# The last attention pair by query halves, and another order of the first and last chains

## The chip, the cores and the metric

The kernel runs on one core of one Trainium2 chip. The metric is the device time of one execution in microseconds. The times shown are of three runs; the profile is of one further execution, with its own time.

A core has five engines that run beside each other and are tied by semaphores: PE (matrix products; its weight loads are listed as PEld), DVE (vector), ACT (scalar functions and copies), POOL (here powers and scalings) and SP (here only the issue of transfers). ACT issues transfers too. Each engine works through its own instructions in order.

## The reference

Eight sequences x[b] of 512 rows with 128 features. All is float32.

```python
x = x + 0.5 * ffn(layernorm(x))
x = x + attention(layernorm(x))
x = x + 0.5 * ffn(layernorm(x))

# attention: 16 heads, rank 64
scores = einsum('bthr,buhr->bthu', x @ Q, x @ K) / sqrt(128)
attn = softmax(scores, axis=3)
return einsum('bthu,bud,hde->bte', attn, x, VO)

# ffn: three blocks, each weight is dequantized 4 bit plus a LoRA product
for blk in range(3):
    y = qlora_linear(h, 2 * blk)
    y = gelu(layernorm(y) * gamma + beta)
    h = qlora_linear(y, 2 * blk + 1) + h
```

## The kernel before

**Pairs and turns.** A batch's 512 rows are four chunks of 128 (c = 0 to 3). Heads go in pairs: 8 pairs per batch, 64 pairs in all, and two pairs make a turn (`lay_turn`), so there are 32 turns. A turn has a nominal length of 32 (`SUP`). For each chunk of queries of a pair: scores on PE (L753), row maxima on DVE (L760), exponentials on ACT with their sums (L765), reciprocals (L772), division by the sums on POOL for one head (L777) and on ACT for the other (L779), and a transpose on DVE (L787) that turns 32x32 blocks into the tile `tr`. The blocks are then moved to their places by 16 transfers from `tr` to `eT` (`exchange`, L802), each 32 partitions by 4 KB. In the last pair (number 63) the odd ones go out on ACT's queue, all others on SP's. The products of `eT` with the values `v` (`attend`, L823) add up in PSUM in `acc0` and `acc1`, over all pairs of a batch; one such product, 128 by 512, is two instructions on PE. They run one or two turns later than the scores of their pair.

**Feed-forward between the turns.** The parts before and after attention of the other batches are laid into the turns by `Unit` and `Block`: a LayerNorm of four chunks at a time (`Norm`: stats L353 and L355 on DVE, root L361 on POOL, scale L366 on DVE, transposes L335 on PE), then for each of three blocks `first` (L388), `biased` (L395 and the stats), root, scale, transposes, `gelu` (L413), `second` (L420), `add` (L426), and at the end `ffn_add` (L436) with the store of the batch.

**The two bare ends.** Where no attention runs beside them, batch 0's first feed-forward part and batch 7's second are done as four `Part` chains, one per chunk: per layer stats (L462), mean (L466), root (L470, POOL), scale (L474), transpose (L479), gelu (L519), and the products into PSUM rows `y` (L490), where all biases and blocks add up. `sum` (L540) ends a part. At the start each part then goes on through a second LayerNorm, its transpose (`keep`, L1025) and its k and q (L700, L706) to the scores of turn 0. Ahead of the end's parts stand copies of `acc0` to `oT` (L1138), transposes (`pot`, L1155) and an addition to x (L537, `xadd`). Pair 61, 62 and 63 are the last three pairs; pair 62's products run after the last turn's scores, then pair 63's.

**The order.** Nothing is scheduled at run time. Every step is put into a list by `at(t, fn)`, the list is sorted by t, and each engine's instructions keep this order by dependencies that the last loop adds. So a number t is a place in the queues, not a time that anything waits for. `START` and `END` hold the t of the bare chains' steps, one number for each of the four parts, relative to `T0` and `E`. A step waits where its data or its buffer are not ready, and all behind it on that engine wait too. PSUM has eight banks of 2 KB per partition, handed out by name (`tag`) from a pool; there are three pools one after the other, and `psum.next` goes to the next.

**Around the change at the end.** With L the place of the last turn, the order on PE is: pair 61's last products and the values of pairs 62 and 63, the transposes `pother` of the half of batch 7's attention sum that lies in `acc1` (its copy on ACT is L854, its addition to x on DVE L860), eight products of pair 62 with `second` and `first` of batch 6's last blocks between them (L + 42 to 45), the transposes of the last block (L + 45.5), four products of pair 63 (L + 58), `second`, three products, the transposes of `ffn_add`, the last product, and then the parts.

**Around the change at the start.** `Unit(0, 1)` and `Unit(0, 2)` are the first feed-forward parts of batches 1 and 2. `lay_start` gets the places of their stats, root, scale, transposes and copy; turn 0 begins at 0.

Of the kernel before, what the change touches and what calls it, by code (L numbers as in the profile page):

```python
# [10 lines left out]
F32 = mybir.dt.float32  # L11
# [7 lines left out]
def kernel(  # L19
# [26 lines left out]
    nc = tc.nc  # L46
# [498 lines left out]
    def part_banks(f):  # L545

        ys = [bank(f"py{f}_{i}", f"y{i}") for i in range(NC)]
        p = [bank(f"pp{f}_{i}", f"g{i}") for i in range(2)]
        return [(ys[i], [p[i % 2][:, 2 * (i // 2) + j, :] for j in range(2)]) for i in range(NC)]
# [107 lines left out]
    class Pair:  # L657
# [123 lines left out]
        def turn(self, c):  # L781

            if c == 0:
                self.tr = work.tile(
                    [P, Q4, 2 * NC, NC, 32], F32, tag="tr", name=f"tr{self.name}", bufs=2
                )
            nc.vector.transpose(  # L787
                self.tr[:, :, :, c, :],
                self.e[c].rearrange("p h (k j r) -> p j (h k) r", j=Q4, r=32),
            )  # L790

        def exchange(self):
# [4 lines left out]
            for s in range(Q4):  # L797
                for i in range(Q4):
                    j = (i + s) % Q4

                    queue = nc.scalar if self.last and i % 2 else nc.sync
                    queue.dma_start(  # L802
# [6 lines left out]
        def attend(self, j, k, tiles):  # L809
# [10 lines left out]
            end = self.g == HP - 1 and k == NC - 1  # L820
# [30 lines left out]
    def lay_other_sum(b, t):  # L851

        a = work.tile([P, NC, P], F32, tag="oT", name=f"other{b}", bufs=2)
        at(t, lambda: nc.scalar.copy(  # L854
            a.rearrange("p c (i q) -> p i c q", q=32), by_chunks(accs[b][1])
        ))

        def add():
            p = transposed(a, f"pother{b}", "g0")
            nc.vector.tensor_tensor(xs[b], xs[b], p, ALU.add)  # L860

        at(t + 3.9, add)
# [3 lines left out]
    def lay_turn(s):  # L866
# [20 lines left out]
        at(t + (24.5 if not last else 22.9), two[1].exchange)  # L887
# [37 lines left out]
    def store(b):  # L925
# [4 lines left out]
        "statsn": (3.79, 3.60, 5.17, 5.36),  # L930
        "meann": (4.09, 3.98, 5.55, 5.66),
        "rootn": (4.71, 4.16, 5.73, 6.28),
        "scalen": (5.74, 4.90, 6.34, 6.89),
        "turnn": (6.12, 5.89, 6.98, 7.83),
        "start": (6.43, 6.20, 7.29, 8.18),
        "bias0": (5.68, 5.78, 6.00, 5.57),
        "y0": (6.77, 6.55, 7.94, 8.49),
        "stats0": (7.35, 7.16, 8.66, 8.91),
        "mean0": (7.65, 7.54, 9.10, 9.51),
        "root0": (8.27, 7.72, 9.28, 9.83),  # L940
        "scale0": (9.18, 8.33, 9.89, 10.44),
        "turn0": (10.10, 8.92, 12.12, 11.47),
        "gelu0": (10.55, 9.23, 12.43, 11.78),
        "bias1": (9.99, 8.81, 10.42, 10.88),
        "second": (11.04, 10.21, 12.92, 12.27),
        "sadd": (11.46, 10.77, 13.36, 12.70),
        "y1": (11.90, 11.26, 13.90, 13.14),
        "stats1": (12.32, 11.79, 14.32, 13.69),
        "mean1": (12.62, 12.09, 14.62, 14.21),
        "root1": (12.82, 12.27, 14.94, 14.39),  # L950
        "scale1": (13.88, 13.03, 15.55, 15.08),
        "turn1": (14.48, 13.47, 16.10, 15.62),
        "gelu1": (14.79, 13.78, 16.41, 15.93),
        "bias2": (14.81, 13.58, 15.99, 15.52),
        "in2": (14.59, 13.68, 16.20, 15.73),
        "y2": (15.29, 14.27, 17.07, 16.42),
        "stats2": (15.88, 14.70, 17.55, 16.84),
        "mean2": (16.43, 15.00, 17.85, 17.14),
        "root2": (16.61, 15.49, 18.03, 17.32),
        "scale2": (17.22, 16.10, 18.64, 17.93),  # L960
        "turn2": (17.88, 16.64, 19.12, 18.37),
        "gelu2": (18.19, 16.95, 19.43, 18.68),
        "bias3": (17.66, 17.28, 19.66, 19.02),
        "in3": (17.77, 16.96, 19.77, 18.91),
        "o31": (17.98, 16.75, 19.45, 18.48),
        "o32": (18.69, 17.44, 19.92, 19.23),
        "sum": (19.16, 18.26, 20.42, 19.79),
        "statsa": (19.60, 18.97, 20.86, 20.23),
        "meana": (20.12, 19.49, 21.32, 20.75),
        "roota": (20.30, 19.67, 21.50, 20.93),  # L970
        "scalea": (21.05, 21.40, 22.11, 21.67),
        "turna": (21.44, 21.79, 22.59, 22.06),
        "keep": (21.75, 22.52, 22.95, 22.37),
        "k": (22.16, 22.91, 23.26, 22.70),
        "kk": (22.80, 23.42, 23.67, 23.12),
        "sc75": 4.40, "w0": 4.62, "w12": 6.01, "w345": 7.73, "cols": 4.70, "colsk": 5.01,
        "gb": 7.73, "gbk": 8.33, "lbA": 3.00, "lbAk": 3.52, "lbB": 6.23, "lbBk": 6.75,
        "wt0": 5.25, "wt0k": 5.77, "wt12": 7.09, "wt12k": 7.93, "wt345": 9.02, "wt345k": 10.19,
        "nat3": 11.58, "nat3a": 12.13, "x21": 12.49, "x21k": 12.91, "cst": 10.71, "cstk": 10.97,
        "qt": 8.34, "qtk": 8.65, "kt": 8.70, "ktk": 9.01, "q": 22.38, "qk": 23.27,  # L980
    }
    T0 = -23.98
# [71 lines left out]
    m.lay_start((-3.3, -2.9, -1.6, 1.95, 5.3), "g0")  # L1054
# [5 lines left out]
    m.lay_start((-1.5, -1.4, 6.2, 9.5, 9.5), "g1")  # L1060
# [4 lines left out]
    for b in range(B):  # L1065
# [10 lines left out]
        if b < B - 1:  # L1076
# [6 lines left out]
                ("first", 2): (44.4, 44.5, 45.0, 45.4),  # L1083
                ("second", 2): (13.5, 13.6, None, 27.7, 27.8),
                "end": 28.9,
# [128 lines left out]
```

## Time and profile before

| | us |
|---|---|
| median of 3 runs | 1083.18 |
| lowest, highest | 1082.44, 1084.1 |
| profiled execution, its time | 1082.74 |
| profiled execution, span from first to last instruction | 1080.9 |
| mean granted clock of PE | 0.997 of full |

| stretch of the trace (us) | PE busy | DVE busy | ACT busy | POOL busy | granted clock |
|---|---|---|---|---|---|
| 22.00 to 25.10 | 3.10 | 2.83 | 1.37 | 1.69 | 1.00 |
| 25.10 to 27.10 | 0.05 | 1.94 | 0.00 | 0.69 | 1.00 |
| 27.60 to 31.20 | 3.52 | 2.54 | 2.13 | 1.19 | 0.59 |
| 1038.90 to 1047.70 | 8.73 | 2.66 | 1.89 | 0.00 | 1.00 |
| 1054.70 to 1061.00 | 6.19 | 1.44 | 0.07 | 0.00 | 1.00 |

Busy time is the time in which an engine had an instruction of its own under way; PE's instructions overlap, so a busy PE is not PE at its peak. The granted clock is the share of full speed at which PE was allowed to run. The chain of waits is the work that ended last, followed back from the last instruction, each step to what released it. The page puts 34% of it on the products of L823 (`acc`), 17% on the scores, 9% on the values.

### The profile page before, as it was taken

How to read it: one execution, taken by the hardware profiler on the slowest of the kernel's cores; microseconds unless marked ns; L12 is line 12 of the kernel's file. 1: busy time of each engine (PE TensorE's matmuls, PEld its weight loads, DVE VectorE, ACT ScalarE, POOL GpSimd, SP SyncE). 2: the span in 40 equal slices, each digit the busy share in tenths (PEclk: the TensorE clock that was granted, in tenths of full speed). 3: DMA queues.
4: the chain of work that ended last, by engine and by line, in shares of the span. 5: the costliest groups of instructions: out<-in, count | busy, mean ns of one | idle time of the engine just before them, and what ended most of it. 6: DMA issues, size and time to landing. Idle time of an engine off the chain costs nothing.

```text
span 1080.9 us, 15560 instructions
## 1 busy us (share of the span) xinstructions
PE 1059.4 (98%) x4594; PEld 559.5 (52%) x4594; DVE 873.4 (81%) x1765; ACT 793.7 (73%) x1710; POOL 485.5 (45%) x368
## 2 busy tenths in 40 slices
PE   8899999999999999999999999999999999999988
PEld 6445544545555554555555455554555554445445
DVE  6798877888788888888889888888978888787745
ACT  4877777777777787777787777787777778776742
POOL 4554334444443454444445444454444344434323
PEclk9999999999999999999999999999999999999999
DMA  6066655665576554566545566555557655566660
GB/s 186 18 143 153 156 121 126 142 142 128 122 166 156 125 117 113 127 155 156 135 113 127 122 139 156 134 133 122 117 130 166 140 127 124 125 141 140 151 156 20
DMA packets 57803, 142.39 MB, mean 132 GB/s; under 512 B 18476, under 2 KB 22648, under 8 KB 57720
## 3 DMA queue, kind: packets, MB, share of 16 engines
q1 hardware_dynamic: 55736, 139.94, 56.4%
q10 hardware_dynamic: 1984, 1.45, 0.6%
q8 instruction: 38, 0.62, 0.2%
q14 instruction: 45, 0.37, 0.1%
HBM read 5.01 MB, written 2.10 MB: 7 GB/s over the span
## 4 chain that ended last, share of the span: by engine, by line
PE 81%; ACT 8%; DVE 7%; issue 1%; SPq 1%; DMA 1%; POOL 0%; DVEq 0%; ACTq 0%; POOLq 0%
PE acc L823 34%; PE ps L753 17%; PE pv L713 9%; PE pqk L690 8%; ACT e L765 5%; PE po L420 4%; PE py L388 3%; DVE tr L787 3%; DVE nm L760 3%; PE py L490 2%; PE p L335 2%; SPq L802 1%; ACT L413 1%; ACT e L779 1%; ACT v L726 1%
## 5 line engine op out<-in xcount | busy, mean ns | idle before, releaser
L777 POOL TENSOR_SCALAR e<-e,rden 128x512 f32<-128x512 f32 x257 | 400.2, 1567 | 336.4 <-DVE rden L772 336.3
L823 PE MATMUL acc<-eT,v 64*128 64x512 f32 (+1 forms) x1768 | 465.6, 591 | 0.5 <-issue 0.4
L765 ACT ACTIVATE e<-ps,nm 128x512 f32<-128x512 f32 x512 | 344.9, 685 | 160.2 <-DVE nm L760 153.4
L787 DVE STREAM_TRANSPOSE tr<-e 128x1024 f32<-128x1024 f32 x256 | 312.8, 1231 | 33.0 <-POOL e L777 24.4
L760 DVE TENSOR_REDUCE nm<-ps 128x2 f32<-128x1024 f32 x256 | 299.8, 1207 | 49.0 <-PE ps L753 48.9
L823 PEld LDWEIGHTS acc<-eT,v 64*128 64x128 f32 (+1 forms) x1768 | 196.4, 188 | 220.0 <-issue 217.8
L753 PE MATMUL ps<-qk 64*128 64x512 f32 x1024 | 248.7, 599 | 4.7 <-ACT e L765 2.9
L779 ACT ACTIVATE e<-e,rden 128x512 f32<-128x512 f32 x255 | 176.2, 726 | 12.4 <-DVE rden L772 10.9
L753 PEld LDWEIGHTS ps<-qk 64*128 64x128 f32 x1024 | 94.2, 186 | 130.6 <-issue 88.2
L713 PE MATMUL pv<-vo_sb,axT 128*128 128x256 f32 x512 | 121.6, 380 | 0.0
L361 POOL TENSOR_TENSOR rstd<-mv,mhalf 128x4 f32<-128x4 f32 x42 | 42.9, 1022 | 151.8 <-DVE mv L355 151.0
L713 PEld LDWEIGHTS pv<-vo_sb,axT 128*128 128x128 f32 x512 | 94.9, 190 | 28.1 <-issue 13.2
L765 ACT ACTIVATION_READ_ACCUMULATOR e<-ps,nm 128x1 f32 x512 | 103.9, 203 | 0.0
L726 ACT COPY v<-pv 128x512 f32<-128x512 f32 x124 | 66.9, 596 | 47.5 <-PE pv L713 47.5
L772 DVE RECIPROCAL rden<-den 128x2 f32<-128x2 f32 x256 | 39.8, 159 | 35.9 <-ACT e L765 35.0
L696 ACT COPY qk<-pqk 128x1024 f32<-128x1024 f32 x61 | 61.0, 1000 | 3.9 <-PE pqk L690 3.9
L690 PE MATMUL pqk<-axT,qT_w 128*128 128x512 f32 x122 | 63.0, 598 | 0.2 <-ACT e L765 0.2
L690 PE MATMUL pqk<-axT,kT_w 128*128 128x512 f32 x122 | 62.3, 592 | 0.0
L426 DVE SCALAR_TENSOR_TENSOR hT<-po,cols,hT 128x512 f32<-128x512 f32 x42 | 30.9, 736 | 23.3 <-PE po L420 22.4
L388 PEld LDWEIGHTS py<-wT,hT 128*128 128x128 f32 x336 | 42.7, 191 | 12.2 <-DVE hT L426 8.4
L395 DVE TENSOR_TENSOR y<-py,bias_bc 128x512 f32<-128x512 f32 x42 | 28.5, 679 | 25.1 <-PE py L388 24.9
L366 DVE TENSOR_SCALAR z<-y,mv,rstd 128x128 f32<-128x128 f32 x168 | 47.6, 355 | 1.2 <-POOL rstd L361 1.2
(136 smaller groups left out, 718.3 us busy)
## 6 DMA issues: line engine op xcount, KB each, us to landing
eT<-tr SPq DMA_DIRECT2D x1016, 128.0 KB, 2.3
x<-in_L_attn_x_dram SPq DMA_DIRECT2D x7, 256.0 KB, 5.0
out_dram<-x SPq DMA_DIRECT2D x7, 256.0 KB, 2.4
eT<-tr ACTq DMA_DIRECT2D x8, 128.0 KB, 3.9
qk_sb<-in_L_attn_Q_dram SPq DMA_DIRECT2D x1, 448.0 KB, 4.1
qk_sb<-in_L_attn_K_dram SPq DMA_DIRECT2D x1, 448.0 KB
x<-in_L_attn_x_dram SPq DMA_DIRECT2D x2, 128.0 KB, 2.7
q_i<-in_L_ffn_qweights_dram SPq DMA_DIRECT2D x1, 192.0 KB, 2.6
```

The lines of the kernel that those rows point to most:

```text
L388: nc.tensor.matmul(self.py[:, c, :], lhsT=hTs[self.b][:, c, :], rhs=wT[:, 2 * self.k, :], start=True, stop=True,)
L690: nc.tensor.matmul(self.pg[:, i, :], lhsT=(qT_w, kT_w)[i][:, self.g, :], rhs=xTs[self.b], start=True, stop=True,)
L696: nc.scalar.copy(self.qk, self.pg)
L713: nc.tensor.matmul(p, lhsT=xTs[self.b][:, c, :], rhs=vo_sb[:, 2 * self.g : 2 * self.g + 2, :], start=True, stop=True,)
L726: nc.scalar.copy(self.v[:, c : c + NC // 2], self.pv[:, c : c + NC // 2])
L753: nc.tensor.matmul(ps[:, j, :], lhsT=self.qk[rows, 0, ts(c, P)], rhs=self.qk[rows, 1, :], start=True, stop=True,)
L760: nc.vector.tensor_reduce(self.nm[:, c, :], self.ps[c], AX.X, ALU.max, negate=True)
L765: nc.scalar.activation(e[:, j, :], self.ps[c][:, j, :], AF.Exp, bias=self.nm[:, c, j : j + 1], accum_out=self.den[:, c, j : j + 1],)
L777: nc.gpsimd.tensor_scalar(e, e, r, None, ALU.mult)
L779: nc.scalar.activation(e, e, AF.Copy, scale=r)
L787: nc.vector.transpose(self.tr[:, :, :, c, :], self.e[c].rearrange("p h (k j r) -> p j (h k) r", j=Q4, r=32),)
L823: nc.tensor.matmul(accs[self.b][i], lhsT=self.v[rows, k, j, :], rhs=self.eT[rows, :, j * NC + k, :], start=first, stop=end and (j == 1 or ...
```

## The change

Pair 63 is handled by halves of the queries: chunks 0 and 1, then 2 and 3. Each half has its own `tr` tile and `eT` tile, of half the size, taken crosswise from the two tags, and its own 16 transfers of 64 KB (32 partitions by 2 KB), even ones on SP, odd ones on ACT. The second half's `eT` tile is claimed after the first half's transfers are issued. The products of pair 63 no longer add to `acc0`; each half has its own PSUM bank (`sum0`, `sum1`) and eight products of 256 columns. What lies in `acc0` and `acc1` is added on DVE and put into x by `pother`, later than before. The last PSUM pool begins ahead of these. The last block of batch 6 (transposes, gelu, `second`, `add`, `ffn_add`) moves behind half 0's products and between half 1's. Parts 0 and 1 need half 0 alone, parts 2 and 3 half 1. `START` and `END` get other numbers throughout, and the stats and roots of `Unit(0, 1)` and `Unit(0, 2)` other places.

```diff
-    def part_banks(f):
+    def part_banks(f, tags=("g0", "g1")):
...
-        p = [bank(f"pp{f}_{i}", f"g{i}") for i in range(2)]
+        p = [bank(f"pp{f}_{i}", tag) for i, tag in enumerate(tags)]
...
         def turn(self, c):
 
+            if self.last:
+                nc.vector.transpose(
+                    self.half_tr(c // 2)[:, :, :, c % 2, :],
+                    self.e[c].rearrange("p h (k j r) -> p j (h k) r", j=Q4, r=32),
+                )
+                return
...
+        def half(self, tag, name):
+
+            h = work.tile(
+                [P, Q4, 2 * NC, P], F32, tag=tag, name=f"{name}{self.name}", bufs=3 - (tag == "tr")
+            )
+            return h.rearrange("p j a q -> p (j a q)")[:, : Q4 * 2 * NC * P // 2]
+
+        def half_tr(self, h):
+            if not hasattr(self, "trs"):
+                self.trs = {}
+            if h not in self.trs:
+                self.trs[h] = self.half(("tr", "eT")[h], f"tr{h}_").rearrange(
+                    "p (j a c r) -> p j a c r", j=Q4, a=2 * NC, c=2
+                )
+            return self.trs[h]
+
+        def exchange_halves(self):
+
+            self.eTs = []
+            for h in range(2):
+                self.eTs.append(self.half(("eT", "tr")[h], f"eT{h}_").rearrange(
+                    "p (i a q) -> p i a q", i=Q4, a=2 * NC
+                ))
+                for n in range(Q4 * Q4):
+                    i = n % Q4
+                    j = (i + n // Q4) % Q4
+                    queue = nc.scalar if i % 2 else nc.sync
+                    queue.dma_start(
+                        out=self.eTs[h][32 * j : 32 * (j + 1), i, :, :].rearrange(
+                            "p a q -> p (a q)"
+                        ),
+                        in_=self.trs[h][32 * i : 32 * (i + 1), j, :, :, :].rearrange(
+                            "p a c r -> p (a c r)"
+                        ),
+                    )
+
+        def attend_half(self, h, p, j, k):
+
+            nc.tensor.matmul(
+                p, lhsT=self.v[:, k, j, :], rhs=self.eTs[h][:, :, j * NC + k, :],
+                start=j == 0 and k == 0, stop=j == 1 and k == NC - 1,
+            )
...
-                    queue = nc.scalar if self.last and i % 2 else nc.sync
-                    queue.dma_start(
+                    nc.sync.dma_start(
...
-            end = self.g == HP - 1 and k == NC - 1
+            end = k == NC - 1 and self.g == HP - (2 if self.b == B - 1 else 1)
...
-    def lay_other_sum(b, t):
+    def lay_other_sum(b, times):
...
-        at(t, lambda: nc.scalar.copy(
-            a.rearrange("p c (i q) -> p i c q", q=32), by_chunks(accs[b][1])
-        ))
-
-        def add():
-            p = transposed(a, f"pother{b}", "g0")
-            nc.vector.tensor_tensor(xs[b], xs[b], p, ALU.add)
-
-        at(t + 3.9, add)
+        by_query = a.rearrange("p c (i q) -> p i c q", q=32)
+        p = []
+        for t, fn in zip(times, (
+            lambda: nc.scalar.copy(by_query, by_chunks(accs[b][1])),
+            lambda: nc.vector.tensor_tensor(by_query, by_query, by_chunks(accs[b][0]), ALU.add),
+            lambda: p.append(transposed(a, f"pother{b}", "g0")),
+            lambda: nc.vector.tensor_tensor(xs[b], xs[b], p[0], ALU.add),
+        )):
+            at(t, fn)
...
-        at(t + (24.5 if not last else 22.9), two[1].exchange)
+        if last:
+            at(t + 22.9, two[1].exchange_halves)
+        else:
+            at(t + 24.5, two[1].exchange)
...
-        "sum": (19.16, 18.26, 20.42, 19.79),
-        "statsa": (19.60, 18.97, 20.86, 20.23),
-        "meana": (20.12, 19.49, 21.32, 20.75),
-        "roota": (20.30, 19.67, 21.50, 20.93),
-        "scalea": (21.05, 21.40, 22.11, 21.67),
...
+        "sum": (18.62, 19.51, 20.34, 21.13),
+        "statsa": (19.32, 19.95, 20.94, 21.57),
+        "meana": (19.84, 20.25, 21.46, 22.03),
+        "roota": (20.02, 20.57, 21.64, 22.21),
+        "scalea": (20.67, 21.76, 22.25, 22.82),
...
-    T0 = -23.98
+    T0 = -24.57
...
-    m.lay_start((-3.3, -2.9, -1.6, 1.95, 5.3), "g0")
+    m.lay_start((-0.9, -0.85, -0.6, 1.95, 5.3), "g0")
...
-    m.lay_start((-1.5, -1.4, 6.2, 9.5, 9.5), "g1")
+    m.lay_start((-0.8, -0.5, 6.2, 9.5, 9.5), "g1")
...
-                ("first", 2): (44.4, 44.5, 45.0, 45.4),
-                ("second", 2): (13.5, 13.6, None, 27.7, 27.8),
-                "end": 28.9,
+                ("first", 2): (44.4, 45.45, 46.0, 46.4),
+                ("second", 2): (27.80, 27.90, None, 30.44, 32.75),
+                "end": 33.56,
...
-        at(t + 26.0 + 0.43 * i, b.attend, i // NC, i % NC, 1)
-    lay_other_sum(B - 1, t - SUP + 21.6)
+    lay_other_sum(B - 1, (t - SUP + 21.6, t + 13.5, t + 22.0, t + 22.1))
+    at(t + 13.51, psum.next)
+    end_sums = []
+    at(t + 13.52, lambda: end_sums.extend(
+        bank(f"sum{h}", f"sum{h}")[:, :2, :].rearrange("p c q -> p (c q)") for h in range(2)
+    ))
+    for i in range(2 * NC):
+        at(t + 20.0 + 0.43 * i, lambda i=i: b.attend_half(0, end_sums[0], i // NC, i % NC))
...
-        "oT": (0.60, 0.20, 0.40, 0.80),
-        "pot": (2.18, 0.57, 1.11, 1.64),
-        "xadd": (3.01, 0.88, 1.51, 1.95),
...
-        "turnn": (5.09, 3.13, 4.03, 4.86),
-        "bias": (2.29, 0.68, 1.21, 1.75),
...
-        "sum": (16.01, 14.03, 14.69, 15.54),
...
+        "oT": (0.20, 0.40, 3.86, 4.21),
+        "pot": (0.97, 0.86, 4.30, 4.83),
+        "xadd": (1.50, 1.17, 4.61, 5.24),
...
+        "turnn": (4.19, 3.65, 7.09, 7.39),
+        "bias": (3.76, 5.16, 4.41, 5.80),
...
+        "sum": (17.24, 17.57, 18.09, 18.57),
+        "attend": (0.00, 0.43, 1.07, 1.50, 1.93, 2.36, 2.79, 3.22),
...
-    for c in sorted(range(NC), key=lambda c: END["oT"][c]):
-        at(E, lambda c=c: nc.scalar.copy(
-            oT[c].rearrange("p (i q) -> p i q", q=32), by_chunks(accs[B - 1][0])[:, :, c, :],
+    for c in range(NC):
+        at(E + END["oT"][c], lambda c=c: nc.scalar.copy(
+            oT[c].rearrange("p (i q) -> p i q", q=32),
+            by_chunks(end_sums[c // 2], 2)[:, :, c % 2, :],
         ))
+    for i in range(2 * NC):
+        at(E + END["attend"][i], lambda i=i: b.attend_half(1, end_sums[1], i // NC, i % NC))
...
-    at(E + 0.01, psum.next)
-    at(E + 0.02, lambda: end_banks.extend(part_banks(1)))
+    at(E + 0.41, lambda: end_banks.extend(part_banks(1, ("g0", "sum0"))))
```

## The prediction

> **What bounds the kernel.** First the page:
>
> ```profile
> span 1080.9 us, 15560 instructions
> PE 1059.4 (98%) x4594; PEld 559.5 (52%) x4594; DVE 873.4 (81%) x1765; ACT 793.7 (73%) x1710; POOL 485.5 (45%) x368
> ```
>
> PE is busy 98% of the span, and the page's chain that ended last lies on PE for 81%. The 31 turns in the middle are full of PE work and lose none of it to this change, so the change is worth what it moves at the two ends, where PE waits. A microsecond saved ahead of turn 0 should come through to the end: the loads from HBM are over by about 22 us (DMA share 0.01 after that), so nothing later hangs on absolute time.
>
> Next, the chain of waits around the end of the first feed-forward part (start, duration, engine, tile, line):
>
> ```profile
> 25.16 0.29 DVE x L540
> 25.46 0.78 DVE sts L353 x4
> 26.24 0.30 DVE mv_n L355 x4
> ...
> 26.75 0.43 POOL prstd L470
> 27.18 0.09 issue
> 27.27 1.02 POOL rstd_n L361
> 28.28 0.52 POOL prstd L470
> 28.80 0.03 issue
> 28.82 0.36 DVE pz L474
> ...
> 31.49 1.06 PE ps L753 x4
> ```
>
> The four parts' own chain ends with sum, stats, mean, root, scale (L540 to L474). Between them stand L353, L355 and L361: the LayerNorm of batch 1, which nobody needs yet. It holds DVE and POOL while every part waits.
>
> The same view at the other end, and PE and clock by stretches (us; busy and count of PE, PEld, DVE, ACT, POOL; granted clock; DMA share; GB/s):
>
> ```profile
> 1038.56 0.41 issue
> ...
> 1045.22 0.91 PE py L388 x8
> ...
> 1048.13 1.04 POOL rstd L361
> ...
> 1049.69 1.01 PE p L335 x4
> 1050.70 0.10 issue
> 1050.79 5.37 PE acc L823 x8
> ...
> 1060.93 0.27 ACT oT L1138
> ```
>
> ```profile
> 1047.70:1049.70 2.00, 0.14 (x2) 0.04 (x1) 0.85 (x7) 0.00 (x0) 1.03 (x1) 1.00 0.44 100
> 1051.50:1054.70 3.20, 3.20 (x5) 1.28 (x4) 0.00 (x0) 0.01 (x1) 0.00 (x0) 0.52 0.02 5
> 1060.90:1078.30 17.40, 15.80 (x104) 12.72 (x104) 13.36 (x56) 7.15 (x20) 8.67 (x16) 1.00 0.07 23
> ```
>
> PE stands idle for 2 us while the last block of batch 6 goes through bias, root and scale, because its transpose is queued ahead of pair 63's products. When these start, the clock is 0.52 and the first eight instructions (four products) take 5.37 us instead of 3.45. Only when all eight are done do four parts start together, and for 17.4 us PE, DVE and POOL share their rows. The last sum ends at 1078.31, the span 2.6 us later with the store.
>
> **The start.** The edit moves batch 1's stats and root (L353, L355, L361), and batch 2's, behind the parts' scales. From the timeline: o32 of the last part ends at 25.14; sum to 25.45; a mean 0.1; stats to 25.8; a scale of another part 0.3; mean to 26.25; root 0.55 (L470, mean 549 ns) from 26.3 to 26.85; scale from 26.9 to 27.25. It was 28.82 to 29.18: 1.9 earlier. Behind it, by the 0.27 to 0.48 rows: transpose, copy, k product, copy to 28.5, the rest of q (0.65) on PE, first scores at 28.9 instead of 31.4.
>
> What is late next is DVE: both batches' stats (0.87 + 0.31 each, 2.35) and batch 1's scale (1.11) now stand between the last part's scale and the first maximum: 27.25 + 2.35 + 1.11 = 30.7, where scores would have allowed 30.0. The first maximum was at 32.60, so the gain is 1.9. Bounds: 2.6 if DVE finds room earlier; zero if the new order of the 5.4 to 25.1 us stretch loses that much. That stretch has the same instructions as before, and PE is busy for 3.10 of 3.10 us in 22.00 to 25.10 and about as much in the slices from 6 us on. Reordering can neither shorten PE's work nor, without new idle time, lengthen it; I take 0, between -0.5 and +1.5. Take 1.9 in all.
>
> **The end, transfers.** The rows of the queues and of the last block transpose of pair 63 (L787):
>
> ```profile
> 1026.88 20.66 SPq L802 DMA_DIRECT2D eT<-tr  x24
> 1037.37 1.25 DVE L787 STREAM_TRANSPOSE tr<-e 128x1024 f32<-128x1024 f32 x1 [1.32 <-ACT e L779]
> 1040.86 4.96 ACTq L802 DMA_DIRECT2D eT<-tr  x5
> ```
>
> Pair 62's 16 transfers go out on SP alone every 0.63 us, the last at 1036.53. Pair 63's 16 (8 on SP, 8 on ACT) wait for the transpose ending at 1038.62 and fill the DMA engines (share about 1.0, 242 to 277 GB/s) until 1048.6. Now they are 32 of half the size, 16 on each queue. Half 0's data are there after the second transpose (about 1034.3); it also needs pair 61's buffer, free when its products end at 1036.4. So ACT can start at about 1036.5, at the latest at 1038.65 as now, SP at 1037.1. A 64 KB transfer of this shape is not in the trace. Lower bound: by bytes, 2 MB at 265 GB/s, 7.9 us. Upper bound: a queue is held as long as for a whole one with both queues active (SP 8.23 us for 7 steps, 1.18). I take SP's lone pace, 0.63, the row nearest to a queue that is limited by its own issue. Half 0 then lands at 1037.1 + 8 x 0.63 + 2.4 = 1044.5, half 1 at 1049.6. Behind the 16 issues on ACT stand the last block's gelu and the sum's copies, wanted at 1052; ACT is free at about 1047. Half 1's second tile takes pair 62's tr buffer, whose readers land at 1038.9, before SP reaches it at 1042: no wait.
>
> A rule of the Trainium skill (DMA: Bandwidth & Descriptors, Bandwidth, Measured) speaks against halving: it gives 138 GB/s for 64 KB transfers and calls smaller ones descriptor-dominated. That page measured other queues and HBM reads; at its rate 2 MB would take 15.2 us, half 1 would land near 1054.5 and the sum would lose some 2 us.
>
> **The end, engines.** PE's order is now: pair 62's eight products with the block's second and first between, half 0's eight, the transposes of the other sum, the block's transposes, two of half 1, the block's second, two part transposes, six of half 1. Pair 62's products start when its transfers land, 1038.97; ACT's early issues may crowd the last two, take +0.3 (0 to 0.6). The stretch to 1047.7 keeps its length: 1048.0. A half product has 256 columns; L713 gives 1.73 for 8 such instructions, two make a product: 8 x 0.43 = 3.45, to 1051.5. They cost no more than the whole ones and fill the 2 us hole. Other sum's and block's transposes, 0.44 each: 1052.35. The block's scale, ready at 1050.35 plus 0.3 and perhaps the 0.7 of DVE's new addition, is hidden by half 0's products.
>
> Then two products (0.86) to 1053.2, gelu (0.78) to the same time, second 0.86 to 1054.1. On ACT the copies of parts 0 and 1 queue behind gelu: 1053.2 to 1053.7. Their two transposes to 1054.35, six products to 1056.95. Part 2's copy comes at 1057.0; the block's final transposes, bias and part transposes bring part 3's to about 1058.7. On DVE stand ffn_add, part 2's addition and stats, then the last addition to x at 1059.4. Before, it was at 1063.62, and 14.7 us later its sum ended; the first part took 14.5. With 14.7 the last sum ends at 1074.1: 4.2 gained, 2.0 of it the hole and 1.9 the clock, the rest the overlap of parts 0 and 1 with half 1, net of the moved 2 x 0.44 + 0.86. Bounds: the row's 104 PE instructions over 15.80 us, begun at 1054.1 with 3.0 of products and transposes, end no earlier than about 1072.9 (5.4 gained); a late half 1 within the transfers' bounds costs the other way.
>
> On the clock, the row is: idle 1047.7 to 1049.7, and 0.52 from 1051.5; at the start idle 25.1 to 27.1, and 0.55 to 0.59 until 31.2. The skill's page (TensorE: Matmul & The Clock Gate, Part 1) asks for an idle window of about 3.4 us. By that rule a 2 us hole would not slow PE and filling it would save 2.0, not 3.9; the trace decides.
>
> **Sum.** 1.9 + 4.2 = 6.1. The profiled execution took 1082.74 (span 1080.9 and 1.84 around it), so 1076.6; the median of the runs is 0.44 higher, so about 1077.0.
>
> **Rivals.**
> - Start eaten: both moves happen, but the reordered parts make PE wait in 6 to 25 us for 1.9 in all. For it: in-order queues, and DVE next in line. Against: PE's rows there have no holes to lose. 1083.2 - 4.2 = 1079.0.
> - Transfers late for half 0: it lands when the whole did, near 1049.7. PE idles 1.7 us from 1048, the clock falls, 1.9 more: the end gains 0.6. For: DMA engines full until 1048.6. Against: half 0 comes first in both queues and has 1 MB. 1083.2 - 2.5 = 1080.7 to 1081.3, by the clock's length.
> - The change doesn't do what it says: PSUM's banks, taken over 20 us earlier, or the buffers put half 0 back behind all, and the start's order gives nothing: 1083.
> - Slower, the other side: each half transfer holds its queue as long as a whole one. 16 x 1.18 from 1037.1 and 2.4 give 1058.4 for half 1. PE waits from 1052.35, in order, with the block's second and all parts behind it; after 6 us of idling it runs at half clock, two products and second take 3.4, and the six others end near 1065 instead of 1057: 8.4 lost, 4.2 slower at the end, 1.9 gained at the start: 1085.5. It decides from a landing past 1058; up to 1052.35 it costs nothing.
>
> **Numbers.** Forecast 0.62, with its own range 1074.5 to 1079; start eaten 0.14; late half 0 0.12; nothing done 0.05; slower 0.07. Within 0.2% (1081.0 to 1085.3, about what a measurement of this kernel can tell from no change) fall the fourth and half the third. Faster 0.82, same 0.10, slower 0.08. The range leaves out the slow end and the nothing case: 1074.0 to 1081.5.
>
> **What would show it.** First maximum near 30.7, batch 1's L353 after the last L474 of the parts. No PE hole and clock 1.00 from 1039 to 1057. Half products at 0.43. Half 1 landed before 1052 on the old clock (1050 on the new). Last addition to x 4 us earlier against the span's end of turn 31, the part chain 14 to 15 us. A hole ahead of either half's products, a DMA pace above 0.8 us per queue, or a part chain above 17 us would make it wrong.

## The result, and the profile after

The changed kernel took 1077.7 us (median of 6 runs, 1076.03 to 1082.29), the kernel before 1083.06 us in the same comparison (6 runs, 1080.62 to 1088.06). The ratio is 0.9957 with a 95% interval of 0.9936 to 0.9978: faster by 0.2 to 0.6%. The forecast was 1077.0. The profiled execution took 1076.29; its page begins:

```profile
span 1074.5 us, 15620 instructions
PE 1054.2 (98%) x4610; PEld 559.4 (52%) x4610; DVE 874.8 (81%) x1766; ACT 793.5 (74%) x1710; POOL 485.6 (45%) x368
```

The span is 6.4 us shorter (1080.9 before), PE's busy time 5.2 us. To see where, the span is cut at two places that every version has: the start of the first row maximum (L760) and the start of the last one.

| us | before | after | difference |
|---|---|---|---|
| start: to the first maximum | 32.6 | 29.5 | 3.1 |
| middle: first to last maximum | 998.1 | 998.0 | 0.1 |
| end: last maximum to the end of the span | 50.2 | 47.0 | 3.2 |

The middle is a pure shift. What the start saves arrives whole at the end.

The start, in the chain of waits of the kernel after (start, duration, engine, tile, line):

```profile
24.27 0.19 DVE x L540
24.46 0.11 DVE pmv L466
...
24.70 0.56 POOL prstd L470
...
25.29 0.36 DVE pz L474
...
25.69 0.33 PE pp L479
...
28.18 1.06 PE ps L753 x4
```

Between the last part's sum and its scale there is no L353, L355 or L361 any more; scores start at 28.18 instead of 31.49. The LayerNorm of batch 1 now stands behind, as the timeline of DVE shows (start, busy time, line, operation, tiles):

```profile
26.13 0.86 DVE L353 BATCH_NORM_STATS2 sts<-x 128x6 f32<-128x128 f32 x4
...
28.42 1.12 DVE L366 TENSOR_SCALAR z_n<-x,mv_n,rstd_n 128x128 f32<-128x128 f32 x4
29.45 1.22 DVE L760 TENSOR_REDUCE nm<-ps 128x2 f32<-128x1024 f32 x1
```

The scores of the first chunk are done at 29.24; the maximum waits 0.2 us for DVE, which was named as next.

The end, in the chain of waits of the kernel after. The new offset to the old profile is 3.2 us (last maximum at 1027.5 instead of 1030.7):

```profile
1032.70 2.30 DMA eT<-tr
1035.00 1.10 issue
1036.10 2.81 PE acc L870 x6
...
1048.40 2.03 DMA eT<-tr
1050.43 0.14 issue
1050.57 1.10 PE sum L836 x4
...
1057.49 0.19 DVE x L537
...
1071.56 0.29 DVE end L540
```

Half 1's last transfer was issued at 1048.40 and landed at 1050.43, and PE took it up at once. The windows of the same kernel (us; busy and count of PE, PEld, DVE, ACT, POOL; granted clock; DMA share; GB/s):

```profile
1045.10:1050.50 5.40, 4.57 (x24) 3.85 (x24) 2.45 (x8) 0.76 (x2) 1.03 (x1) 1.00 0.48 116
...
1055.40:1071.80 16.40, 14.93 (x106) 12.45 (x104) 12.27 (x49) 6.77 (x18) 7.61 (x14) 1.00 0.07 25
```

The old hole of 2 us and the clock of 0.52 behind it are gone. But PE lacks 0.83 us in the first stretch: a smaller hole, ahead of half 1, which was not forecast. The four parts' stretch is 16.4 us instead of 17.4.

### The profile page after: what moved, and what is told of

Same layout as the page of the kernel before. It is cut to its first block, busy times and chain, and to the rows that moved or that the text cites. A ratio compares the mean times of both kernels' runs of the same rounds, so it can differ in the third digit from the quotient of the medians.

```text
span 1074.5 us, 15620 instructions
## 1 busy us (share of the span) xinstructions
PE 1054.2 (98%) x4610; PEld 559.4 (52%) x4610; DVE 874.8 (81%) x1766; ACT 793.5 (74%) x1710; POOL 485.6 (45%) x368
## 4 chain that ended last, share of the span: by engine, by line
PE 79%; ACT 8%; DVE 7%; SPq 2%; issue 1%; DMA 1%; POOL 0%; DVEq 0%; ACTq 0%; POOLq 0%
PE acc L870 33%; PE ps L753 17%; PE pqk L690 9%; PE pv L713 8%; ACT e L765 5%; PE po L420 4%; PE py L388 3%; DVE tr L793 3%; DVE nm L760 2%; SPq L849 2%; PE p L335 1%; PE py L490 1%; ACT L413 1%; DMA eT<-tr 1%; ACT e L779 1%
## 5 line engine op out<-in xcount | busy, mean ns | idle before, releaser
L870 PE MATMUL acc<-eT,v 64*128 64x512 f32 (+1 forms) x1752 | 456.6, 590 | 1.2 <-issue 1.2
L760 DVE TENSOR_REDUCE nm<-ps 128x2 f32<-128x1024 f32 x256 | 299.8, 1207 | 46.9 <-PE ps L753 46.7
L793 DVE STREAM_TRANSPOSE tr<-e 128x1024 f32<-128x1024 f32 x252 | 307.9, 1231 | 31.9 <-POOL e L777 23.9
L870 PEld LDWEIGHTS acc<-eT,v 64*128 64x128 f32 (+1 forms) x1752 | 193.4, 187 | 216.2 <-issue 213.6
L361 POOL TENSOR_TENSOR rstd<-mv,mhalf 128x4 f32<-128x4 f32 x42 | 42.9, 1022 | 152.1 <-DVE mv L355 151.3
L726 ACT COPY v<-pv 128x512 f32<-128x512 f32 x124 | 66.9, 596 | 47.0 <-PE pv L713 47.0
L395 DVE TENSOR_TENSOR y<-py,bias_bc 128x512 f32<-128x512 f32 x42 | 28.5, 679 | 25.3 <-PE py L388 25.0
L388 PE MATMUL py<-wT,hT 128*128 128x128 f32 x336 | 45.0, 277 | 1.0 <-DVE hT L426 0.8
```

Of the source, the lines that this page charges most:

```text
L388: nc.tensor.matmul(self.py[:, c, :], lhsT=hTs[self.b][:, c, :], rhs=wT[:, 2 * self.k, :], start=True, stop=True,)
L726: nc.scalar.copy(self.v[:, c : c + NC // 2], self.pv[:, c : c + NC // 2])
L760: nc.vector.tensor_reduce(self.nm[:, c, :], self.ps[c], AX.X, ALU.max, negate=True)
L793: nc.vector.transpose(self.tr[:, :, :, c, :], self.e[c].rearrange("p h (k j r) -> p j (h k) r", j=Q4, r=32),)
L870: nc.tensor.matmul(accs[self.b][i], lhsT=self.v[rows, k, j, :], rhs=self.eT[rows, :, j * NC + k, :], start=first, stop=end and (j == 1 or ...
```

## The experiments

All versions compute the whole result; e11 adds transposes that nothing reads. "First maximum", "middle" and "end" are the three stages of the table above; the runs of a group shared their runs of the kernel before.

| run | span | first maximum | middle | end | first change of the clock | clock at half | times |
|---|---|---|---|---|---|---|---|
| before | 1080.9 | 32.6 | 998.1 | 50.2 | 10.1 | 27.2 to 30.6, 1051.2 to 1054.6 | 1083.06, n 6 |
| after | 1074.5 | 29.5 | 998.0 | 47.0 | 5.1 | no | 1077.7, n 6 |
| e1 start only | 1078.9 | 32.3 | 998.0 | 48.6 | 4.6 | 8.1 to 14.9 | 1081.35, n 10 |
| e2 end only | 1076.6 | 30.8 | 998.2 | 47.6 | 4.9 | 25.4 to 28.8 | 1079.68, n 10 |
| e3 LayerNorm only | 1076.9 | 30.3 | 998.0 | 48.6 | 9.8 | no | 1078.70, n 1 |
| e4 order only | 1085.6 | 36.4 | 999.1 | 50.1 | 14.3 | 31.4 to 38.2, 1055.4 to 1058.8 | 1087.42, n 1 |
| e5 after again | 1077.8 | 32.3 | 998.1 | 47.4 | 4.6 | 8.0 to 14.8 | 1080.36, n 11 |
| e6 block only | 1079.4 | 31.7 | 998.2 | 49.5 | 9.2 | no | 1081.24, n 1 |
| e7 half 0 early | 1073.6 | 29.3 | 998.1 | 46.2 | 5.1 | no | 1075.39, n 1 |
| e8 early, 11 and 5 | 1074.0 | 29.7 | 998.1 | 46.2 | 5.3 | no | 1076.42, n 6 |
| e9 e7, timed | 1073.6 | 29.3 | 998.1 | 46.2 | 5.1 | no | 1078.69, n 6 |
| e10 e7, old order | 1072.6 | 28.4 | 997.9 | 46.3 | 4.9 | no | 1076.29, n 6 |
| e11 e7, longer warm-up | 1074.6 | 30.3 | 998.0 | 46.3 | 5.3 | no | 1076.65, n 5 |
| e12 before again | 1080.8 | 34.0 | 998.3 | 48.5 | 9.7 | 26.8 to 33.6 | 1082.61, n 1 |

"Clock at half" leaves out the last 1.5 us, behind PE's last work. The trace's record of the granted clock begins with its first change; the views print 1.00 for the time before it. In e4 PE does 17 instructions in the 3.4 us before that moment and 26 in the 3.4 us behind it, with PE busy all the time, so the first change is where full pace begins.

Two things are read off before any single run. The middle is 997.9 to 998.3 in all but e4 (999.1). And the first maximum of one and the same program moves by up to 2.8 us between profiles (after and e5: 29.5 and 32.3), so a difference of 1 us at the start in one profile is not evidence.

### e1 and e2: each end alone

```diff
 e1: before, with the new START, T0 and
+    m.lay_start((-0.9, -0.85, -0.6, 1.95, 5.3), "g0")
+    m.lay_start((-0.8, -0.5, 6.2, 9.5, 9.5), "g1")
 e2: after, with the old START, T0 and
+    m.lay_start((-3.3, -2.9, -1.6, 1.95, 5.3), "g0")
+    m.lay_start((-1.5, -1.4, 6.2, 9.5, 9.5), "g1")
```

> The kernel before with the changed kernel's START table, T0 and the two lay_start lines; the end as before. Theory (each end is worth what its own stretch shows): first row maximum near 29.5 us instead of 32.6, span 1080.9 - 3.2 = 1077.7, end stretch from the last scores to the last sum as long as before (48.8 us). Rival (the turns give the start's gain back, the end made all of it): first maximum early but span 1080 or more.

> The changed kernel with the old START table, T0 and lay_start lines. Theory: first maximum at 32.6 as before, the end as in the changed kernel, span 1080.9 - 3.2 = 1077.7. Rival (the end's gain needs the early start, or there is none): span above 1080.

Measured against the kernel before: e1 0.9976 (0.996 to 0.9992), e2 0.9969 (0.9957 to 0.9982). Each end is a gain by itself: 2.6 us (0.9 to 4.3) and 3.4 us (1.9 to 4.7) of 1083. Their sum, 6.0, agrees with the 4.7 us (2.4 to 6.9) of the whole change in its first comparison and lies above the 2.4 (1.2 to 3.7) of the second (e5), so the times don't say that the ends add up exactly. The stages do: the new end takes 47.0 to 47.6 with either start (after, e2, e5).

In the profiles the stages say something else than expected. e1's first maximum is at 32.3 and not near 29.5, because PE ran at half clock from 8.1 to 14.9 us; and its end is 48.6 although its end is the old one. e2's first maximum is at 30.8 and not at 32.6: with the same start as the kernel before, its clock came up at 4.9 us instead of 10.1. The windows and the chain of e1 show why:

```profile
1047.30:1049.30 2.00, 0.15 (x1) 0.02 (x1) 0.85 (x7) 0.00 (x0) 1.03 (x1) 1.00 0.50 113
1050.40:1054.10 3.70, 3.69 (x9) 1.79 (x10) 0.00 (x0) 0.74 (x1) 0.00 (x0) 1.00 0.03 7
```

```profile
1050.41 3.67 PE acc L823 x8
```

The same 2 us hole is there, but the clock stays at 1.00 behind it, and the eight instructions take 3.67 us instead of 5.37. So 1.7 us of the old end were the clock, and it does not fall in every execution.

### e3 and e4: the two parts of the start

```diff
 e3: before, with only the two new lay_start lines
 e4: before, with only the new START and T0
```

> The kernel before with only the two lay_start lines changed: the LayerNorms of batches 1 and 2 go behind the parts' scales, the order of the parts stays. Theory (the prediction's step): the last scale of the parts comes right after its own root, first maximum 32.6 - 1.9 to 2.2, near 30.5, PE's clock stays up between 25 and 31 us. Rival (the new order of the parts made the gain): first maximum above 32.

> The kernel before with only the START table and T0 changed; the LayerNorms of batches 1 and 2 stay between the parts' steps. Theory (the order of the first 25 us is worth about 1.0, by PE reaching full pace near 7 us instead of 10): last sum of the parts near 24.2 instead of 25.2, first maximum near 31.6. Rival (PE's pace in the first 10 us is a matter of chance, not of the order): PE's pace turns at 10 us and the last sum stays at 25.2, first maximum near 32.6.

e3's first maximum is at 30.3: 2.3 earlier than before, and the chain of waits shows the same link closed as in the kernel after:

```profile
25.02 0.29 DVE x L540
...
25.64 0.26 DVE pz L474
...
25.94 0.93 PE pp L479 x3
...
29.00 1.06 PE ps L753 x4
```

The sum of the part ends at 25.3, as before (25.45); what is shorter lies behind it, and the first 10 us of the two profiles agree. e4 went far off: its first maximum is at 36.4. The windows of e4 and of the kernel before, both from 8.00 to 14.50 us (columns as above):

```profile
8.00:14.50 6.50, 6.50 (x29) 5.40 (x29) 2.66 (x11) 2.29 (x8) 1.65 (x3) 1.00 1.09 310
```

```profile
8.00:14.50 6.50, 6.50 (x43) 5.40 (x41) 3.86 (x14) 3.46 (x11) 2.83 (x6) 1.00 0.97 295
```

PE is busy all the time in both, but e4 gets 29 instructions done and the kernel before 43. (The two orders mix long and short products differently, so a part of the difference can be the mix; the weight loads shown in the last section tell the pace itself.) Then the clock falls as well, from 31.4 to 38.2 us, with the LayerNorm in its old place. So e4 does not price the order of `START`: it measures a slow PE, and neither of the two expected numbers came (31.6, 32.6). What the new order alone brings at full pace is not shown. That it isn't needed is shown by e3, which has the old one.

### e5 and e6: the change again, and the moved block without the halves

```diff
 e5: after, unchanged
 e6: before, with
+        at(t + 20.0 + 0.43 * i, b.attend, i // NC, i % NC, 1)
+                ("second", 2): (27.3, 27.4, None, 27.7, 27.8),
```

> The changed kernel once more. Theory (the middle is fixed, the two ends vary with the clock that PE is granted): first to last row maximum 998.0 to 998.2 us again, from the last maximum to the end of the span 47.0 where the clock stays up, and the first maximum anywhere from 29.5 to 32.5, by the moment at which PE reaches full pace in the first 12 us. Rival (29.5 belongs to the new order): first maximum within 0.3 of 29.5.

> The kernel before, with pair 63 whole as it was, but its eight products ahead of the last block's transposes and gelu; second and add stay behind. Theory (the block's gelu and add need products to hide behind, and only the halves leave some): from the last maximum to the end of the span 48.3 to 48.9, as before where the clock stays up (48.6). Rival (moving the block is the whole gain, the halves add nothing): 47.3 or less.

e5's ratio is 0.9978 (0.9966 to 0.9989). Its start was the slow one:

```profile
4.00:8.00 4.00, 3.62 (x18) 2.06 (x18) 3.51 (x17) 1.81 (x8) 2.14 (x4) 1.00 0.65 165
8.00:14.50 6.50, 6.50 (x28) 5.44 (x27) 3.27 (x13) 2.69 (x9) 2.58 (x4) 0.50 1.03 295
```

```profile
8.00:14.50 6.50, 6.50 (x48) 5.46 (x47) 4.54 (x18) 3.84 (x13) 3.19 (x6) 1.00 1.03 304
```

The second fence is the kernel after, first profile: the same program, 48 instructions instead of 28 in the same 6.5 us. That is the whole difference of the two first maxima: DVE's steps are 0.1 us earlier in e5 up to 8.2 us and 2.8 later from 16.4 us on, and they stay so. It does not explain all slow runs of this kernel. Of its 17 runs 12 took over 1079, up to 1082.37, and only two of these, 1079.56 and 1079.05, have a lowered mean clock (0.996); the others have 0.999 or 1.000. A late first change as in e4 would not lower that mean, since the record begins with it, but none of those runs has a profile, so their cause is not shown.

e6 puts pair 63's whole products ahead of the last block. Its end is 49.5, 0.9 worse than an old end without the clock's fall (48.6), and later than both its expectations. The chain of waits of e6:

```profile
1046.13 2.33 DMA eT<-tr
...
1048.60 7.10 PE acc L823 x16
1055.70 0.45 PE p L335 x4
...
1056.18 0.79 ACT aT L413
...
1057.01 1.14 PE po L420 x2
...
1058.17 0.76 DVE hT L426
```

The hole is not filled: PE waits 1.6 us for the whole transfers, which land at 1048.46, and so the products start about where the old hole ended. They then run without a break, but from L335 on each step of the block waits for the one before, alone: gelu, second, add. So the halves do two things: a first half lands early enough to fill the hole, and the second one's products are what the block hides behind. Moving the block alone gains nothing. The halves without the moved block were not run.

### e7, e8 and e9: half 0's transfers earlier

In the kernel after, half 1 landed late. The timeline of ACT and of both queues shows where the transfers started (ACTq and SPq are the issues):

```profile
1029.93 3.99 SPq L849 DMA_DIRECT2D eT<-tr  x6
...
1035.24 0.60 ACTq L825 DMA_DIRECT2D eT<-tr  x1
1035.84 0.78 ACT L413 ACTIVATE aT<-p,gb 128x512 f32<-128x512 f32 x1
...
1036.52 1.06 ACT L726 COPY v<-pv 128x512 f32<-128x512 f32 x2
...
1037.32 11.68 SPq L825 DMA_DIRECT2D eT<-tr  x16
```

SP was free at 1033.9, when it had issued pair 62's last one, and yet it started at 1037.32. The program's own list of instructions with their waits gives the reason (number, line, what, waits; the tile names shortened to `eT`, `tr`, `v`, `pv`):

```
ACT 1180 L726 TensorCopy v<-pv    [waits PE]
ACT 1182 L825 DMACopy    eT<-tr   [waits DMAHW4, 5, 3, 6, 2, 7, 1, 0]
SP  1036 L849 DMACopy    eT<-tr   [waits DMAHW3]
SP  1037 L825 DMACopy    eT<-tr   [waits DMAHW6, DVE, PE]
```

In this program eight completion semaphores (DMAHW0 to 7) serve both queues in turn, in the order of the list. Counted through, ACT's first half transfer holds number 6, and SP's first half transfer, eight places later, needs the same number: it waits until ACT's has landed, at 1037.24. What its other two waits stand for was over: half 0's transposes on DVE by 1032.84, pair 61's last products on PE by 1033.18. And ACT's first stands behind the value copy L726, which waits for PE's last values product, ended 1034.91. The theory: put half 0's transfers ahead of those copies, and both queues start 1 to 2 us earlier. The rival: the pace of the transfers, or SP's larger share, sets the landing.

```diff
-            at(t + 22.9, two[1].exchange_halves)
+            at(t + 21.9, two[1].exchange_half, 0)
+            at(t + 22.9, two[1].exchange_half, 1)
 e8 besides:
-                    queue = nc.scalar if i % 2 else nc.sync
+                    queue = nc.scalar if i % 2 or h and n in (6, 10, 14) else nc.sync
```

> The changed kernel with the first half's transfers placed ahead of the last two copies of values on ACT. Theory (ACT's first transfer waits behind those copies, which wait for the last values on PE, and SP's first waits until ACT's first has landed because they share a semaphore): ACT's first transfer goes out about 6 us after the last maximum instead of 7.7, SP's first at its landing, near 8.2 instead of 9.8, half 1 is there about 1.5 earlier, PE's wait of 0.87 ahead of it goes, end stretch 46.1. Rival (the DMA engines or the eight semaphores set the pace): half 1 lands 22.9 after the last maximum as now, end stretch 47.0.

> As the run before it, and three of SP's transfers of half 1 go to ACT (11 and 5). Theory (SP is the last to finish, 3.5 us behind ACT): half 1 lands another 1 to 2 us earlier, 20 after the last maximum, end stretch 46.0, since only PE's 0.87 was to be had; faster than the changed kernel by 0.9. Rival: the eight semaphores tie the queues, half 1 lands no earlier and the end stretch stays at 47.0.

> The kernel of e7 again, timed. Theory (the end is worth 46.2 whenever the clock stays up there, the start 29.3 or 32.3 by the clock): span near 1073.5 or 1076.5, median some 1 us below the changed kernel, ratio to the kernel before 0.994 to 0.997. Rival (e7's time was the lucky start alone): median 1080 as in e5.

The end of e7 is 46.2, 0.8 less than after. The same timeline and the windows of e7:

```profile
1033.13 0.60 ACTq L826 DMA_DIRECT2D eT<-tr  x1
...
1036.30 10.65 SPq L826 DMA_DIRECT2D eT<-tr  x16
...
1036.44 2.81 PE L871 MATMUL acc<-eT,v 128*128 128x512 f32 x6 [1.62 <-DMA eT<-tr]
```

```profile
1045.10:1049.60 4.50, 4.50 (x26) 3.95 (x25) 2.80 (x11) 0.00 (x0) 1.03 (x1) 1.00 0.25 63
1049.60:1055.00 5.40, 5.40 (x28) 4.06 (x27) 2.44 (x10) 1.36 (x4) 1.08 (x2) 1.00 0.00 0
```

ACT starts 2.1 earlier, SP 1.0 (1.6 was expected). In e7's list SP's first half transfer has the number of ACT's second, which landed at 1036.22, and SP went at 1036.30, so the shared semaphore holds here too. PE has no hole left from half 0's first product to the last of half 1. Against the last maximum, pair 62's products start some 0.4 later than after: ACT's early transfers crowd pair 62's last ones, as was feared at 0.3, and it costs less than the late half 1 did. e8 moves three of SP's transfers to ACT. Half 1 landed no earlier (21.0 after the last maximum in both), so the 1 to 2 us of its theory did not come, and its end is 46.2 too: with no hole left there was nothing for the balance to win. The end repeats in e9 (46.2). The timed ratios are 0.995 (0.9934 to 0.9967) for e8 and 0.9962 (0.9947 to 0.9976) for e9. Both lie beside 0.9957 for the kernel after (0.9978 in e5): 0.8 us is less than what the start does to a median.

### e10 and e11: what the start still holds

```diff
 e10: e7, with the old START and T0 (the lay_start lines stay new)
 e11: e7, with
-    at(T0 + 1.5, busy, 10)
+    at(T0 + 1.5, busy, 16)
```

> The kernel of e7 with the old START table and T0, but the new places of the LayerNorms of batches 1 and 2. Theory (the new order of the parts adds nothing; what differs from run to run is the clock): first maximum 30.3 with the late full pace as in e3, down to 28.5 with the early one, end 46.2, span 1073 to 1075, median not above that of e9. Rival (the order is worth 0.8 or more): first maximum 30.3 or later whatever the clock, median 0.8 or more above e9.

> The kernel of e7 with 16 instead of 10 transposes of the identity ahead of the first products, whose results nothing reads. Theory (PE's pace in the first 12 us follows how busy PE was shortly before): PE reaches full pace by 5.5 us and keeps it, first maximum 29.5 to 30.3 in spite of some 0.8 us that the added work holds back the first products, and no time above 1078. Rival (the clock's fall at 8 us does not depend on it): falls as in e1 and e5, first maximum up to 33.2.

e10's first maximum is at 28.4, 0.9 earlier than e7's and e9's, with PE at the same pace (49 instructions in 8.00 to 14.50, 47 in e7). Its ratio, 0.9947 (0.9931 to 0.9964), is the best of all, at 1076.29 us. It overlaps those of e8, e9 and the first of the kernel after, so that it beats them is not shown. What is shown is that the new order of the parts isn't needed for the gain. e11's longer warm-up of PE puts the first maximum at 30.3 and gives 0.9953 (0.9937 to 0.9969): no gain to be seen. Its theory also had no time above 1078, and one of the five runs took 1081.11.

### e12: the kernel before again

> The kernel before once more. Theory (the clock at both ends is a matter of the execution, not of the program): first to last maximum 998.0 to 998.2, first maximum anywhere from 30.8 to 36, and the end 48.6 where the clock stays up behind PE's hole of 2 us, 50.2 where it falls. Rival (this program's clock always falls there): 32.6 and 50.2 again.

The windows and the chain of e12:

```profile
1049.20:1051.20 2.00, 0.17 (x1) 0.00 (x0) 0.84 (x7) 0.00 (x0) 1.03 (x1) 1.00 0.52 117
1052.30:1056.10 3.80, 3.74 (x9) 1.82 (x10) 0.00 (x0) 0.75 (x1) 0.00 (x0) 1.00 0.02 4
```

```profile
1052.36 3.67 PE acc L823 x8
```

The hole of 2 us again, and no fall of the clock behind it: the end is 48.5, as in e1 and e3. At the start the clock did fall, from 26.8 to 33.6, and the first maximum came at 34.0.

## Why the prediction was right, and where it was not

The span was predicted to shrink by 6.1 and shrank by 6.4 between the two profiles. The sum held because two errors of about 1 us have opposite signs: the start gained 1.2 more than predicted, the end 1.0 less. That is luck. In the second comparison (e5) the median of the changed kernel was 1080.36, outside the range of 1074.5 to 1079 that the forecast itself was given.

| step | predicted | measured |
|---|---|---|
| LayerNorm of batch 1 moved | 1.9 | 2.3 (before to e3) |
| new order of the parts | 0, from -0.5 to +1.5 lost | not separable; 0.9 lost in e7 and e9 against e10 |
| PE's pace ahead of the parts | not in the sum | 0.8 gained in this profile (e3 to after), 2.0 lost in e5, the new order included |
| end: the clock | 1.9 | 1.6, in two of five profiles of the old end |
| end: the hole and the overlap | 2.3 | 1.0 to 1.6; 2.4 in e7 |

**The LayerNorm.** Right in mechanism, 0.4 too small. The hole in PE from 25.1 to 27.1 closes (0.95 us of it stay in e3), and with it the fall of the clock behind it, which the working did not count at the start: with the LayerNorm in its old place the clock fell between 25 and 39 us in four of five profiles (before, e2, e4, e12; not e6), in its new place in none of nine. DVE is next in line, as said: first maximum predicted at 30.7, measured at 30.3 in e3.

**The order of the parts.** "Reordering can neither shorten PE's work nor, without new idle time, lengthen it" assumed that PE's work has one length. It has not: 28 and 48 instructions of the same program in the same 6.5 us, all busy. That was the largest unknown of the start, and it was left out of the sum. e1, e4 and e5 of eight profiles with the new order were slow until 14 to 15 us. Of six with the old order four (before, e3, e6, e12) were slow until 9 to 10 us and none longer. Whether the order has part in this stays open; the kernel before also had runs up to 1088.06, and those have no profile.

**The hole and the clock at the end.** The hole of 2 us was filled, as said. The fall of the clock was taken from the one profile as if every execution had it. Of five profiles with the old end's products, two had it (before 50.2, e4 50.1) and three not (48.6, 48.6, 48.5). The forecast against the profiled execution could count 1.9 there, one against the median could not. The clock has part in the median all the same. In the experiments' comparisons the mean granted clock was 0.997 in 41 and 0.998 in 9 of 50 runs of the kernel before; 0.003 of 1081 us are 3.2 us. In 15 of 17 runs of the changed kernel it was 0.999 or 1.000. Where in a run the clock fell, this mean does not say. In e1, which has the old end but not the start's hole, 8 of 10 runs are at 1.000, so the end alone seldom made it fall there.

**The transfers, the step that failed.** The text let SP go at 1037.1, 1033.9 on the new clock; it went at 1037.32, 3.4 later. ACT's start was within its bounds (1033.3 to 1035.45; measured 1035.24). What was overlooked is that ACT's issue stands behind the value copies and that SP's waits for ACT's landing. The pace was nearly right: an issue of 64 KB takes 0.59 to 0.60, and SP needed 0.73 per transfer with its waits, against 0.63. Half 0 had been given 3.5 us in hand and lost them all (PE waited 0.18), half 1 landed at 1050.43 where 1046.4 was predicted, and PE waited 0.87 (1.2 in e5, 1.4 in e2). The prediction itself had named a hole ahead of either half's products as a sign of being wrong, and half 1 was to land before 1050 on the new clock. e7 shows the cause: with both queues started earlier the waits are gone, and the end's 2.4 us without the clock are the 2.3 of the forecast.

The Trainium skill's rate for 64 KB transfers (DMA: Bandwidth & Descriptors, Bandwidth, Measured) had been set aside. Two MB at its 138 GB/s are an estimated 15.2 us, and from the first issue to the last landing it was 1050.43 - 1035.24 = 15.2. The number agrees, but in this trace it is made up of SP's late start (2.1), 16 issues at 0.73 and 1.4 from the end of the last issue to its landing; that the transfers themselves are held to the page's rate no run here shows. The price put on it, 2 us, was too high, since PE lost 1.05 in all.

**The rest.** Pair 62's products were to start at 1036.1 on the new clock (1036.10); a half product costs 0.43 (2.59 for twelve instructions, six products); the last addition to x came at 1057.4 where 1056.2 was predicted, 1.2 late by half 1; and the chain behind it took 14.45 against 14.7.

**The rivals.** "Start eaten" fell in this profile (3.1 gained at the start), though e5, at 32.3, is what it describes, by another mechanism: not a wait but PE's pace. "Half 0 late" did not come: it was late by 0.18 and the clock stayed up. "Slower" needed 1.18 us per half transfer; it was 0.73. "Nothing done" is refuted by e1 and e2.

## What to carry to other kernels

When transfers are halved, look at what releases the first issue on each queue, not at the pace alone: an issue on a compute engine's queue stands behind that engine's waits, and shared completion semaphores carry its delay to the other queue. Before summing from one profile, ask which of its terms (a fall of the clock, the pace of PE in the first 15 us) would come back in a second profile of the same kernel. A block that is moved off the path needs independent work behind which to wait; count that work first.

## What was not expected of the hardware

- PE's pace in the first 15 us is not set by the program alone. The same kernel did 48 or 28 PE instructions between 8.00 and 14.50. In e5 the granted clock says so (0.50); in e4 it reads 1.00 with 29 instructions, since the record begins at 14.3. The groups by line of PE's weight loads from 8 to 13 us, first of the kernel after, then of e4, show the same load (number, busy time, mean ns) at two speeds, so a granted clock of 1.00 this early in the record doesn't mean full speed:

```profile
L490 PEld LDWEIGHTS py<-ident,cols 128*128 128x128 f32 x4 | 0.5, 137 | 0.0
```

```profile
L490 PEld LDWEIGHTS py<-ident,cols 128*128 128x128 f32 x3 | 0.7, 228 | 0.1
```

- A hole of 2.0 us in PE was followed by a fall of the clock in two of five profiles at the end and in four of five at the start (in e4's start the idle time is in four pieces). The traces show what differs: in each of them the clock changes only on a grid of 3.41 us (in the profile of before at 10.09, 27.15, 30.57, 1051.15 and 1054.57, all whole multiples apart), each fall ahead of the last 1.5 us lasts one or two such stretches, and where the grid begins differs from profile to profile. The table has the share of the stretch with the most of the hole in which PE was busy:

| hole | clock fell in the next stretch | it did not |
|---|---|---|
| start | 0.43 (before), 0.43 (e2), 0.47 (e4), 0.46 (e12) | 0.55 (e6) |
| end | 0.43 (before), 0.45 (e4) | 0.51 (e1), 0.58 (e12), 0.45 (e3) |

Ahead of all six falls the hole lay within one stretch but for 0.1 us at most; in e6 and at the end of e1 and e12 the grid cut off 0.2 to 0.5 us of it, and the clock stayed up. So whether a hole of this length costs anything depended mostly on where the grid lay. The busy share is not the whole rule: e3 is an exception, and in e1 and e5 the clock fell at 8 us behind a stretch in which PE was busy for 0.9. The Trainium skill (TensorE: Matmul & The Clock Gate, Part 1) speaks of a window of about 3.4 us that runs freely, so that the moment of the change varies between runs. These profiles agree; that PE must be idle for a whole window before its clock falls, they do not show, and six of ten holes of 2 us measured here were enough.
- ACT issued its transfer at 1035.24, ahead of the gelu (1035.84) and the value copies (1036.52) that stand before it in its list. What held it was a wait of one of these instructions, not their execution.
